# A two-layer graph transformer on one core: lists loaded in two parts, first loads in order of use, the next layer's k and v over four chunks, attention spread at the border

## The chip, the core and the metric

The kernel runs on one core of a Trainium2 chip. The metric is the device time of one launch in microseconds, the median of several runs. The engines are PE (matrix multiplications; PEld is its loading of weights), DVE (elementwise work and reductions), ACT (activations, copies, scaling), POOL (elementwise work, and the issue of gathers and scatters) and SP (issues loads and stores; ACT issues some too).

## What is computed

x has 2708 rows (tokens) of 512 numbers; adj is a 2708 x 2708 matrix of 0 and 1, symmetric, with ones on its diagonal and a few to some twenty ones in a row. Two layers of the same form follow each other, everything in float32:

```python
mask = adj.astype(jnp.float32) + jnp.eye(n, dtype=jnp.float32)
q = (h @ Wq.T + bq).reshape(n, N_HEADS, D_K)      # k and v alike; 8 heads of 64
scores = jnp.einsum('nhd,mhd->hnm', q, k) / jnp.sqrt(jnp.float32(D_K))
scores = jnp.where(mask[None, :, :] == 0, jnp.float32(-1000000000.0), scores)
attn = jax.nn.softmax(scores, axis=-1)
ctx = jnp.einsum('hnm,mhd->nhd', attn, v).reshape(n, D_MODEL)
h1 = _layer_norm(h + ctx @ Wo.T + bo, ln1_g, ln1_b)
ff = jax.nn.relu(h1 @ W1.T + b1) @ W2.T + b2      # 512 -> 2048 -> 512
h2 = _layer_norm(h1 + ff, ln2_g, ln2_b)
```

## The kernel before

The attention goes by edges: for each token only the rows of k and v at the ones of its adjacency row are gathered. Tokens are sorted by the number of ones, most first, into 22 tiles of 128 ranks (the last has 20); `CAPS` gives how many neighbours each tile needs, 22 for tile 0 and 3 for tile 21. `order` is the order of attention: tiles 21 and 20, 19 and 18, 8 and 9, 7 and 10, 6 and 11, 0 and 17, and so on, two tiles a block, 11 blocks.

**First stage** (`first`, L802). For each tile of tokens, in their own order, PE makes k and v (`project`, L564: four products of 128 x 128 by 512 columns) from columns `xg` of x transposed, loaded 256 tokens at a time into three buffers (L811). Beside it `lists` (L649) finds the ones of each adjacency row: SP loads 1354 KB a tile into one of two buffers, POOL adds the diagonal, ACT writes codes, DVE takes the largest codes in segments (L663 to L670). Then `counted` (L678) and `ranked` (L735) make each token's rank; PE adds up over partitions (L742, L749), 22 scatters on POOL's queue (L768) write each token's list to its rank in `rec_d`, and two loads bring the lists back in order of rank: `back` (L779, 21 tiles) and `rest` (L783, 20 rows). A cast on POOL (L794) makes `ident_i` (which token has each rank), and `listed` (L796), on DVE, `idx` and `minus` (the neighbours and their masks).

**First queries** (`first_queries`, L862). PE makes q of the 22 tiles in token order; after the tenth `listed` runs and the pool `pa`, which holds the lists' work, is given back; after the eleventh PE turns the gathered rows `xr` of the first three rank tiles (L1097) and makes their q; attention begins beside the rest of the queries. A gather of q by rank needs all 22 tiles of q stored.

**Main loop** (L1478). For each block `feed_forward` (L1240) runs 16 chunks f: pf, four products of 256 columns (L1265), ACT's relu to ft (L1273), and, `LAG` = 3 chunks later, two products of 512 columns into a (L1253). Beside it run: the attention of later blocks, in steps that `advance(x)` (L1393) lets through: a step has a cost, a credit of at most 1.5 grows by x, and no step is let through while two finished tiles wait in `got`; `through` (L1403) does what is missing of the next block at f = 10, whose context tiles cx are then turned (L1097), projected (o) and normed (`attended`, L1208); and in layer 0 `keys_values` (L1299), the k and v of the layer after for the block just finished, in four pieces: turn the two tiles; k and v of one; k and v of the other; two scatters (L1324). DVE takes k away (L1316), ACT v (L1318).

An attention step: POOL issues gathers of two neighbours of 128 tokens into one of five kv buffers (L951), DVE multiplies by q and adds up (L988, L994), ACT takes the exponent (L1007) and weighs half of the values (L1014), DVE the other half (L1020) and adds (L1027); at a tile's end DVE sums (L1035 to L1050) and ACT divides (L1058).

**The border** (L1450 to L1470). When layer 0 is done, PE makes the first sixteen tiles of layer 1's q (`query`, L1190, evicted by DVE at L1195), the first eight from preloaded zT, the rest from zT that SP loads (L1182), three buffers ahead, behind the stores of the q's (L1205). The first block's attention is let in between by `advance`.

Accumulators in the tag "g" (k, v, q, o, and turned tiles, `ps`) are three. The order on PE, ACT and SP is written out by hand; so is POOL's in the first stage and layer 0, and DVE's in the first queries and at the border. Elsewhere a scheduler orders DVE and POOL.

Of the kernel before, what the change touches and what calls it, by code (L numbers as in the profile page):

```python
# [8 lines left out]
F32 = mybir.dt.float32  # L9
# [37 lines left out]
EARLY = 3  # L47
PACE = (0.62, 0.72)
# [422 lines left out]
def by_edges(ctx: ExitStack, tc: tile.TileContext, x, xT, adj, layers, out, good):  # L471
# [113 lines left out]
    def lists_of(pa):  # L585
# [49 lines left out]
        new = pa.tile([P, NT, 32], F32, tag="new", name="new", bufs=1)  # L635
# [99 lines left out]
        def ranked(hot, before, half):  # L735
# [30 lines left out]
            for t in range(NT):  # L766
# [12 lines left out]
            back = nc.gpsimd.dma_start(  # L779
                out=new[:, : NT - 1, :],  # L780
                in_=rec_d[: (NT - 1) * P, :].rearrange("(g p) c -> p g c", p=P),
            )
            rest = nc.gpsimd.dma_start(out=new[:LW, NT - 1, :], in_=rec_d[(NT - 1) * P :, :])  # L783
            for load in (back, rest):
# [9 lines left out]
            nc.gpsimd.tensor_copy(ident_i, new[:, :, LIST])  # L794

        def listed():  # L796
            nc.vector.tensor_scalar(idx, new[:, :, :LIST], 1.0, 1.0, ALU.max, ALU.subtract)
            nc.vector.tensor_scalar(minus, new[:, :, :LIST], 0.0, NEG, ALU.is_equal, ALU.mult)
# [3 lines left out]
    def first(w, meanwhile):  # L802
# [3 lines left out]
        def load():  # L806
            i = len(xg)
            b = i % XBS * XB
            bw = min(XB, N - b)
            t = wts.tile([P, NC, XB], F32, tag=f"w1_{5 + i % 3}", name="xg")  # L810
            nc.sync.dma_start(out=t[:, :, :bw], in_=chunked(xT)[:, :, b : b + bw])  # L811
            xg.append(t)

        def tokens(t, again):

            i, c0 = t * P // XB, t * P % XB
            if c0 == 0 and len(xg) < 2 * XBS:
                load()
            xs = xg[i + again * XBS]
            return lambda c: xs[:, c, c0 : c0 + size(t)]  # L820

        cols = given_column(w, "bq"), given_column(w, "bk")
        load()
        wk = matrix(w, "Wk", "wk")
        turning = turned_row(cols[1], "bk", 1.0)
# [5 lines left out]
        for t in range(NT):  # L831
# [14 lines left out]
            if t == 0:  # L846
                load()
# [6 lines left out]
            if t == QT:  # L854
                wq = matrix(w, "Wq", "wq")
                turning = turned_row(cols[0], "bq", DK**-0.5)
# [5 lines left out]
    def first_queries(bq, wq, listed, pa, tokens, meanwhile):  # L862
# [15 lines left out]
        for t in range(NT):  # L878
# [10 lines left out]
            if t == OWN - 1:  # L889
                listed()  # L890
# [6 lines left out]
            if t == OWN:  # L897
                zTs = [turned_own(g, xr) for g, xr in zip(order, xrs)]
                for g, zT in zip(blocks[0], zTs):
                    own_query(g, zT, to[g], bq, wq)  # L900
                    advance(0.5)
            if t == OWN + 2:
# [544 lines left out]
    for n in range(NL):  # L1447
        last = n == NL - 1
        nxt = None if last else Layer(n + 1, layers[n + 1])
        if n > 0:  # L1450
# [3 lines left out]
            with tc.manual_schedule(engines={mybir.EngineType.DVE}):  # L1454
# [4 lines left out]
                while pool:  # L1459
                    advance(1.0)  # L1460
                    now.query(*pool.pop(0))
                for i in range(2 * AHEAD - 10):
                    advance(1.0 if i < 3 else 0.4)
# [14 lines left out]
        for k, block in enumerate(blocks):  # L1478
# [4 lines left out]
            for f, zs in enumerate(now.feed_forward(block, hs, hT)):  # L1483
                if f == NFC:
                    break
                if f in (5, 6) and behind:
                    next(behind)
                    if f == 6:
                        for _ in behind:
                            advance(1.0)  # L1490
                        behind = None
# [125 lines left out]
```

## Time and profile before

| | us |
|---|---|
| median of 5 runs | 1974.93 |
| lowest and highest | 1971.67, 1978.03 |
| the profiled execution, whole | 1970.44 |
| its span, first to last instruction | 1968.7 |
| PE busy | 1897.2 |
| DVE, ACT, POOL busy | 1303.2, 933.2, 794.5 |
| kv gathers on POOL's queue (420), busy | 547.5 |
| mean granted clock of PE | 0.986 |

PE's busy time is a union: a matmul counts from its start to a modelled end, and matmuls overlap. A wait line reads "engine line tile <- engine line: us in total, times, longest us". A timeline row is start, length, engine, line, operation, tiles, shapes, how many, and in brackets the idle time before it and what ended it. The granted clock of PE is 1.00 at full speed. In time the stages are: k, v and lists to about 165 us, first queries to 270, layer 0's blocks to 1160, the border to 1235, layer 1 to the end.

### The profile page before, as it was taken

To read this page: it belongs to the slowest core of one execution; us is meant where nothing else is said; L and a number is where in the kernel's file an instruction comes from. 1 tells how busy PE (TensorE), PEld (TensorE's weight loads), DVE (VectorE), ACT (ScalarE), POOL (GpSimd) and SP (SyncE) were. 2 spreads that over 40 slices of the span, in tenths; PEclk is the share of its full clock that TensorE was granted. 3 is DMA by queue.
4 is the path that set the end of the run, shared out by engine and by line. 5 is a ranking of instruction groups with operands and counts; after the bars stand their busy time and mean duration, and the time that the engine had idled before them with its cause. 6 is when DMAs were issued, how large, how long until landed. Compare 5 with 4: busy or idle time off the path is not lost. (4 is left out here: it accounts for less than half of the span.)

```text
span 1968.7 us, 20843 instructions
## 1 busy us (share of the span) xinstructions
PE 1897.2 (96%) x6150; PEld 1099.8 (56%) x6150; DVE 1303.2 (66%) x2139; ACT 933.2 (47%) x3218; POOL 794.5 (40%) x708
## 2 busy tenths in 40 slices
PE   8999989999999999999999997999999999999997
PEld 3443434465565655666556643556666566666664
DVE  6884587585867959659442035887688988877421
ACT  4560344464555655547332112756456765755310
POOL 3114535462555645425310022555346655544210
PEclk9999989999999999999999998999999999999998
DMA  8998767454645656546310755856455766554100
GB/s 328 353 315 283 246 213 257 150 198 157 210 153 194 208 175 222 170 145 210 127 44 22 230 168 203 286 181 214 156 185 190 251 214 211 183 191 150 37 11 13
DMA packets 130942, 366.92 MB, mean 186 GB/s; under 512 B 16636, under 2 KB 36460, under 8 KB 128110
## 3 DMA queue, kind: packets, MB, share of 16 engines
q0 software_dynamic: 69104, 246.35, 37.6%
q1 hardware_dynamic: 52804, 99.66, 14.7%
q10 hardware_dynamic: 8910, 19.48, 2.6%
q8 instruction: 50, 0.82, 0.2%
q14 instruction: 74, 0.61, 0.1%
HBM read 314.62 MB, written 50.83 MB: 186 GB/s over the span
## 5 line engine op out<-in xcount | busy, mean ns | idle before, releaser
L951 POOL DMA_INDIRECT kv<-kv_d,idx x420 | 547.5, 1303 | 488.9 <-DVE acc L1027 332.2
L1253 PE MATMUL a<-w,ft 128*128 128x512 f32 (+1 forms) x1408 | 666.1, 598 | 9.3 <-ACT ft L1273 9.3
L1265 PE MATMUL pf<-hT,w 128*128 128x256 f32 (+1 forms) x2816 | 635.7, 373 | 10.8 <-ACT ft L1273 8.3
L1265 PEld LDWEIGHTS pf<-hT,w 128*128 128x128 f32 x2816 | 520.9, 191 | 188.8 <-issue 107.8
L1253 PEld LDWEIGHTS a<-w,ft 128*128 128x128 f32 (+1 forms) x1408 | 256.0, 186 | 233.9 <-issue 198.1
L1273 ACT ACTIVATE ft<-pf,b 128x256 f32<-128x256 f32 (+1 forms) x352 | 157.6, 458 | 426.3 <-PE pf L1265 425.8
L988 DVE TENSOR_TENSOR kv<-kv,q 128x1024 f32<-128x1024 f32 (+3 forms) x222 | 256.3, 1157 | 139.3 <-DMA kv<-kv_d,idx 130.5
L1014 ACT ACTIVATE kv<-kv,p 128x64 f32<-128x64 f32 x1232 | 311.0, 335 | 5.0
L994 DVE TENSOR_REDUCE sc<-kv 128x16 f32<-128x1024 f32 (+3 forms) x222 | 254.6, 1152 | 1.1
L1027 DVE TENSOR_TENSOR acc<-acc,kv 128x1024 f32<-128x1024 f32 (+2 forms) x178 | 203.7, 1144 | 35.7 <-ACT kv L1014 35.2
L1087 POOL TENSOR_TENSOR rd<-va,mhalf 128x1 f32<-128x1 f32 (+1 forms) x88 | 85.6, 973 | 278.6 <-DVE va L1085 277.2
L1007 ACT ACTIVATE p<-sc,minus 128x8 f32<-128x8 f32 (+1 forms) x420 | 103.4, 295 | 167.8 <-DVE sc L994 159.9
L1020 DVE TENSOR_TENSOR kv<-kv,p 128x512 f32<-128x512 f32 (+1 forms) x178 | 121.3, 682 | 72.2 <-ACT p L1007 72.2
L568 PE MATMUL o<-wo,cT 128*128 128x512 f32 (+1 forms) x352 | 155.1, 593 | 0.5 <-ACT cT L1102 0.5
L568 PEld LDWEIGHTS o<-wo,cT 128*128 128x128 f32 (+1 forms) x352 | 65.1, 186 | 86.5 <-issue 74.7
L1058 ACT ACTIVATE cx<-acc,su 128x64 f32<-128x64 f32 (+1 forms) x352 | 88.5, 334 | 42.7 <-DVE su L1050 34.7
L1285 DVE TENSOR_TENSOR h<-a,h 128x512 f32<-128x512 f32 (+1 forms) x44 | 29.7, 677 | 106.3 <-PE a L1253 106.1
L1091 DVE SCALAR_TENSOR_TENSOR h<-h,rd,ln_b 128x512 f32<-128x512 f32 (+1 forms) x88 | 65.8, 747 | 49.2 <-POOL rd L1087 49.2
L660 ACT ACTIVATE code<-aj 128x2708 bf16<-128x2708 int32 (+1 forms) x22 | 73.2, 3330 | 47.7 <-POOL aj L656 44.1
L663 DVE MAX8 tops<-code 128x8 f32<-128x247 f32 (+2 forms) x242 | 82.9, 401 | 17.6 <-ACT code L660 17.6
L1014 ACT ACTIVATE acc<-kv,p 128x64 f32<-128x64 f32 (+1 forms) x352 | 88.8, 334 | 1.4
L1324 POOL DMA_INDIRECT kv_d<-kvs,ident_i x22 | 23.1, 1051 | 162.5 <-ACT kvs L1318 95.4
(132 smaller groups left out, 1512.9 us busy)
## 6 DMA issues: line engine op xcount, KB each, us to landing
aj<-in_adj SPq DMA_DIRECT2D x21, 1354.0 KB, 7.3
kv_d<-kvs ACTq DMA_DIRECT2D x21, 512.0 KB, 6.9
xg<-in_xT SPq DMA_DIRECT2D x20, 512.0 KB, 5.8
w<-in_W SPq DMA_DIRECT2D x20, 512.0 KB, 4.8
kv<-kv_d,idx POOLq DMA_INDIRECT x420, 5.6
w<-in_W ACTq DMA_DIRECT2D x12, 512.0 KB, 6.1
q_d<-qs SPq DMA_DIRECT2D x22, 256.0 KB, 3.1
zT_d<-zT SPq DMA_DIRECT2D x22, 256.0 KB, 3.4
```

Source lines behind the costliest of these rows:

```text
L568: nc.tensor.matmul(o[:r], xs(c), wm[:, c, :], start=(c == 0), stop=(c == NC - 1))
L951: nc.gpsimd.indirect_dma_start(out=to, out_offset=None, in_=table[:, :], in_offset=bass.IndirectOffsetOnAxis(ap=s, axis=0), bounds_check=N ...
L988: nc.vector.tensor_tensor(kv[:r, :c, :DM], kv[:r, :c, :DM], self.q[:r].unsqueeze(1).to_broadcast([r, c, DM]), ALU.mult,)
L994: nc.vector.tensor_reduce(self.sc[:r, s0 : s0 + c, :], kv[:r, :c, :DM].rearrange("p s (h d) -> p s h d", d=DK), AX.X, ALU.add,)
L1007: nc.scalar.activation(p[:r, s, :], self.sc[:r, s, :], AF.Exp, bias=minus[:r, g, s : s + 1])
L1014: nc.scalar.activation(to[:, i, hd], kv[:r, i, DM + h * DK : DM + (h + 1) * DK], AF.Copy, scale=p[:r, s0 + i, h : h + 1],)
L1020: nc.vector.tensor_tensor(to[:, 0, :].rearrange("p (h d) -> p h d", d=DK), kv[:r, 0, DM:].rearrange("p (h d) -> p h d", d=DK), p[:r, s0, : ...
L1027: nc.vector.tensor_tensor(self.acc[:r, :c, :], self.acc[:r, :c, :], kv[:r, :c, DM:], ALU.add)
L1058: nc.scalar.activation(cx[:r, hd], self.acc[:r, 0, hd], AF.Copy, scale=self.su[:r, h : h + 1])
L1253: nc.tensor.matmul(a[:r], fts[f][:, c0 : c0 + r], self.w2[f // 2][:, f % 2, :], start=(f == 0), stop=(f == NFC - 1),)
L1265: nc.tensor.matmul(pf[:, :w], self.w1[f // 2][:, c, f % 2 * P : f % 2 * P + P], hT[:, c, :w], start=(c == 0), stop=(c == NC - 1),)
L1273: nc.scalar.activation(ft[:, :w], pf[:, :w], AF.Relu, bias=self.b1[:, f : f + 1])
```

## The change

Five edits. (1) `back` becomes a function and the lists come in three loads: first `rest`, then the three tiles before it, then the other 18; a cast for the last four tiles follows, and `listed` is called twice, for four tiles after the tenth query and for 18 after the twelfth, with a second cast on POOL. (2) Because the lists now outlive the pool `pa`, `new` lies in the buffer of `hT`. (3) The first loads: half of xg (128 tokens), the first quarter of Wk, the column bk, the rest of Wk, the column bq, the other half of xg; before, both columns, all of xg, all of Wk. (4) `keys_values` is stepped once at each of f = 5, 6, 7 and 8; before, once at 5 and all the rest at 6, with three `advance(1.0)` that go. (5) At the border each query or streamed step lets `advance(0.65)` through; before 1.0, and 0.4 from the fourth streamed step on.

```diff
--- before.py
+++ after.py
@@ -45,6 +45,7 @@
 QT = 6
 OWN = 10
 EARLY = 3
+FIRST = 4
 PACE = (0.62, 0.72)
 
 
@@ -632,7 +633,9 @@
             base=0,
             channel_multiplier=-1,
         )
-        new = pa.tile([P, NT, 32], F32, tag="new", name="new", bufs=1)
+        new = dn.tile([P, NC, 2 * P], F32, tag="hT", name="new", bufs=1)
+        new = new.rearrange("p c t -> p (c t)")[:, : NT * 32]
+        new = new.rearrange("p (g c) -> p g c", c=32)
         nc.gpsimd.memset(new, 0.0)
         nc.gpsimd.dma_start(
             out=rec_d[: (NT - 1) * P, :].rearrange("(g p) c -> p g c", p=P),
@@ -776,12 +779,16 @@
                 tc.declare_no_dep(move.ins, group="moved", reason="no two tokens have one rank")
                 tc.add_to_no_dep_group("moved", move.ins)
                 moved.append(move)
-            back = nc.gpsimd.dma_start(
-                out=new[:, : NT - 1, :],
-                in_=rec_d[: (NT - 1) * P, :].rearrange("(g p) c -> p g c", p=P),
-            )
-            rest = nc.gpsimd.dma_start(out=new[:LW, NT - 1, :], in_=rec_d[(NT - 1) * P :, :])
-            for load in (back, rest):
+            def back(a, b):
+                load = nc.gpsimd.dma_start(
+                    out=new[:, a:b, :],
+                    in_=rec_d[a * P : b * P, :].rearrange("(g p) c -> p g c", p=P),
+                )
+                return load
+
+            first, last = NT - FIRST, NT - 1
+            rest = nc.gpsimd.dma_start(out=new[:LW, last, :], in_=rec_d[last * P :, :])
+            for load in (rest, back(first, last), back(0, first)):
                 for move in moved:
                     tc.add_manual_dep(
                         load.ins,
@@ -791,11 +798,16 @@
                         ),
                         reason="every list is in its place",
                     )
-            nc.gpsimd.tensor_copy(ident_i, new[:, :, LIST])
-
-        def listed():
-            nc.vector.tensor_scalar(idx, new[:, :, :LIST], 1.0, 1.0, ALU.max, ALU.subtract)
-            nc.vector.tensor_scalar(minus, new[:, :, :LIST], 0.0, NEG, ALU.is_equal, ALU.mult)
+            nc.gpsimd.tensor_copy(ident_i[:, first:], new[:, first:, LIST])
+
+        def listed(start):
+
+            ts = slice(NT - FIRST, NT) if start else slice(0, NT - FIRST)
+            if not start:
+                nc.gpsimd.tensor_copy(ident_i[:, ts], new[:, ts, LIST])
+            some = new[:, ts, :LIST]
+            nc.vector.tensor_scalar(idx[:, ts, :], some, 1.0, 1.0, ALU.max, ALU.subtract)
+            nc.vector.tensor_scalar(minus[:, ts, :], some, 0.0, NEG, ALU.is_equal, ALU.mult)
 
         return lists, counted, ranked, listed
 
@@ -808,21 +820,32 @@
             b = i % XBS * XB
             bw = min(XB, N - b)
             t = wts.tile([P, NC, XB], F32, tag=f"w1_{5 + i % 3}", name="xg")
-            nc.sync.dma_start(out=t[:, :, :bw], in_=chunked(xT)[:, :, b : b + bw])
             xg.append(t)
+            step = bw if i else P
+            for a in range(0, bw, step):
+                nc.sync.dma_start(
+                    out=t[:, :, a : a + step], in_=chunked(xT)[:, :, b + a : b + a + step]
+                )
+                yield
 
         def tokens(t, again):
 
             i, c0 = t * P // XB, t * P % XB
             if c0 == 0 and len(xg) < 2 * XBS:
-                load()
+                finish(load())
             xs = xg[i + again * XBS]
             return lambda c: xs[:, c, c0 : c0 + size(t)]
 
-        cols = given_column(w, "bq"), given_column(w, "bk")
-        load()
-        wk = matrix(w, "Wk", "wk")
-        turning = turned_row(cols[1], "bk", 1.0)
+        wk = wts.tile([P, NC, DM], F32, tag="wk", name="wk")
+        halves = load()
+        next(halves)
+        for c in range(NC):
+            nc.sync.dma_start(out=wk[:, c, :], in_=chunked(w["Wk"])[:, c, :])
+            if c == 0:
+                cols = [given_column(w, "bk")]
+        cols.append(given_column(w, "bq"))
+        finish(halves)
+        turning = turned_row(cols[0], "bk", 1.0)
         bk = next(turning)
         wv = matrix(w, "Wv", "wv")
         pa = tc.tile_pool(name="pa", bufs=2)
@@ -844,7 +867,7 @@
                 nc.scalar.dma_start(**before)
             before = dict(out=kv_d[0][t * P : t * P + r, :], in_=kv[:r])
             if t == 0:
-                load()
+                finish(load())
             while done < min(NT, 1 + LEAD * t):
                 lists(done)
                 done += 1
@@ -853,7 +876,7 @@
             meanwhile(t)
             if t == QT:
                 wq = matrix(w, "Wq", "wq")
-                turning = turned_row(cols[0], "bq", DK**-0.5)
+                turning = turned_row(cols[1], "bq", DK**-0.5)
                 bq = next(turning)
                 finish(turning)
         nc.scalar.dma_start(**before)
@@ -887,7 +910,7 @@
                 qs[:r, t % 2], q[:r], DK**-0.5, bq[:r], ALU.mult, ALU.add
             )
             if t == OWN - 1:
-                listed()
+                listed(True)
                 pa.__exit__(None, None, None)
                 at = ctx.enter_context(tc.tile_pool(name="at", bufs=2))
                 for g in order[:3]:
@@ -899,6 +922,8 @@
                 for g, zT in zip(blocks[0], zTs):
                     own_query(g, zT, to[g], bq, wq)
                     advance(0.5)
+            if t == OWN + 1:
+                listed(False)
             if t == OWN + 2:
                 own_query(order[2], zTs[2], to[order[2]], bq, wq)
             meanwhile(t)
@@ -1457,10 +1482,10 @@
                 next(ahead)
                 next(streamed)
                 while pool:
-                    advance(1.0)
+                    advance(0.65)
                     now.query(*pool.pop(0))
                 for i in range(2 * AHEAD - 10):
-                    advance(1.0 if i < 3 else 0.4)
+                    advance(0.65)
                     next(streamed)
                 through(0)
                 early[n] = now.attended(blocks[0], got)
@@ -1483,12 +1508,8 @@
             for f, zs in enumerate(now.feed_forward(block, hs, hT)):
                 if f == NFC:
                     break
-                if f in (5, 6) and behind:
+                if f in (5, 6, 7, 8) and behind:
                     next(behind)
-                    if f == 6:
-                        for _ in behind:
-                            advance(1.0)
-                        behind = None
                 if more and f == 10 + (k + n == 0):
                     through(k + 1)
                     projecting = now.attended(blocks[k + 1], got)
```

## The prediction

> **What bounds the kernel now.** I read the busy row of the page first, then the list of who waited for whom on the matmul engine, then the table by stretches of time, and last the timelines around the longest waits. The busy row:
>
> ```profile
> PE 1897.2 (96%) x6150; PEld 1099.8 (56%) x6150; DVE 1303.2 (66%) x2139; ACT 933.2 (47%) x3218; POOL 794.5 (40%) x708
> ```
>
> PE does something 96% of the span, so 1968.7 − 1897.2 = 71.5 us are idle, 13 of them the store at the end. No other engine is near full over the span. The time can only go where PE stands still, or where it runs at a lower clock. The waits of PE, longest in total first:
>
> ```profile
> PE a L1253 <- ACT ft L1273: 9.3, 9, 2.8
> PE q L568 <- DVE qs L1195: 8.7, 2, 5.9
> PE pf L1265 <- ACT ft L1273: 8.3, 3, 5.9
> PE v L568 <- DVE kvs L1316: 6.4, 2, 4.6
> PE k L568 <- DMA wk<-in_Wk: 6.3, 1, 6.3
> ...
> PE tp L1097 <- DMA xr<-in_x,ident_i: 3.5, 3, 2.7
> PE pr L742 <- DVE kvs L838: 3.4, 1, 3.4
> ```
>
> Four of these are touched: the start (6.3), the first lists (3.5), the next layer's k and v (6.4), the queries at the border (8.7). The table by stretches shows what stands beside them; columns: stretch, length, then busy time of PE, PEld, DVE, ACT, POOL, the granted clock of PE, DMA share and rate.
>
> ```profile
> 155.00:170.00 15.00, 11.61 (x31) 4.19 (x30) 8.91 (x33) 0.91 (x2) 3.98 (x4) 1.00 0.77 263
> 204.00:220.00 16.00, 12.45 (x32) 4.69 (x31) 3.79 (x4) 1.56 (x4) 10.95 (x11) 0.79 0.72 218
> 371.00:383.00 12.00, 7.40 (x13) 3.04 (x12) 5.73 (x8) 0.75 (x2) 0.94 (x1) 0.72 0.12 41
> 1186.00:1207.00 21.00, 11.36 (x18) 4.18 (x16) 14.66 (x23) 5.13 (x21) 7.91 (x6) 0.76 0.67 235
> ```
>
> After three of the four waits the clock falls (0.79, 0.72, 0.76) and the matmuls that follow take longer, so a wait costs more than its own length. After the wait of 3.39 us at 158 it stayed at 1.00. Rows of the timelines:
>
> ```profile
> 195.10 1.50 POOL L779 DMA_DIRECT2D new<-rec_d  x1 [1.65 <-DMA rec_d<-rec,ranks]
> 203.19 0.48 POOL L794 CAST ident_i<-new 128x22 int32<-128x22 f32 x1 [6.02 <-DMA new<-rec_d]
> 207.86 0.58 PE L1097 MATMUL tp<-ident,xr 20*128 20x20 f32 x4 [2.70 <-DMA xr<-in_x,ident_i]
> 376.58 6.21 PE L568 MATMUL v<-wv,zT 128*128 128x512 f32 x8 [4.60 <-DVE kvs L1316]
> 375.85 1.26 DVE L1316 TENSOR_TENSOR kvs<-k,bk 20x512 f32<-20x512 f32 x2
> 1200.57 5.53 PE L568 MATMUL q<-wq,zT 128*128 128x512 f32 x8 [5.88 <-DVE qs L1195]
> 1199.88 1.82 DVE L1195 SCALAR_TENSOR_TENSOR qs<-q,bq 128x512 f32<-128x512 f32 x3
> ```
>
> A projection is 3.44 us from start to start at the full clock (k at 149.83 to v, and on); the 6.21 and 5.53 above are the same work at the lower clock. In the built order of both programs PE has the same instructions; only the k and v of the second tile of each layer-0 block move behind one feed-forward chunk.
>
> **First loads.** Before, two columns (0.79 and 1.24) stand ahead of the 512 KB of xg (1.71) and of Wk (2.18); PE starts at 6.34. Now half of xg is first at 0.79: 0.92 us sooner, and 256 KB less ahead of the first matmul, 0.8 us at the 328 GB/s of slice 1 of the page: PE starts near 4.6, some 1.7 us sooner. SP issues one DMA more (0.4 us) ahead of the adjacency loads; the bytes ahead of them are the same. That does not reach the end: at 158.25 PE waits for the list chain on DVE (L838 and what stands ahead of it), whose adjacency loads keep DMA at 0.90 to 0.93. An earlier PE only waits longer, 3.39 + 1.7 − 0.5 = 4.6 us. I give the chain 0.5 us from DMA having started sooner (bounds −0.4, the extra issue, and 0.9). The longer wait may now bring the clock down: nothing by the 3.39 row, 6.21 − 3.60 = 2.6 us by the 4.60 row; I take 1.2, about midway, as 4.6 equals the one length but the other is the same place. Together 0.5 − 1.2: 0.7 us lost.
>
> **Lists.** The cast waits for one load of 336 KB and one of 2.5 KB behind it, until 203.19. Now 2.5 KB (issue 0.58) and 48 KB (at most 0.7) go first, then 288 KB (at most 1.5); the cast wants the first two but stands behind the third's issue, so not before 195.10 + 2.8 = 197.9. Landing of the short ones: between the 3.5 us of a gather of xr and the 6.5 us that the 2.5 KB load took, so 195.10 + 1.3 + 3.5 to 6.5 = 199.9 to 202.9, since the queue's neighbours (q_d, xg) load DMA just then. I take 200.2, nearest to xr, which goes through the same queue beside the same loads: 3 us sooner. The three xr land 3 us sooner, the last near 207.2; PE arrives at 205.16 and waits about 1 us instead of 3.55, and the loss by clock goes mostly: from 205.16 to 219.96 are 14.8 us for 0.3 + 2 × 0.43 + 2 × 3.44 = 8.0 us of work, 6.8 lost. I take 5.0 won, less 0.6 because the second part of the lists puts 0.8 us of DVE (432 of the 528 columns of 0.44 + 0.45) in the stretch 224 to 242 that ends at PE's `tp<-cx` at 244.09 without slack. 4.4 us; bounds 0 (the load lands no sooner) and 6.8. POOL's second cast (0.4) stands behind four gathers; its load has long landed.
>
> The Trainium skill, DMA: Bandwidth & Descriptors, section "Anatomy of one DMA — SWDGE (gpsimd) path", speaks against this part: it puts a load at about 2.0 us fixed plus bytes over 436 GB/s, so 336 KB would take 2.8 us and 48 KB 2.1, an estimate of 0.7 us saved, and the whole sum would be some 4 us smaller. The rows here (7.8 us for the 336 KB, 6.5 for 2.5 KB behind it) do not follow it, so I keep to them.
>
> **k and v of layer 1.** There are three accumulators under the tag of k and v, so the second v waits until the first k is taken away by DVE L1316 at 375.85 to 376.5. DVE is held there by gathers (waits of 6.32, 0.92 and 0.36 us for kv before it), not by PE. With a chunk (pf and a, 3.44 us) between, PE reaches that v at 375.4 and waits 1.1 us. Before, from the end of the second k at 371.98 to 382.63 are 10.65 us for 3.44 of work; after, 1.1 + 3.44 when the clock holds: 6.1 us won. DVE's chain behind it moves by only about 3 us (it waits for ACT's p, which waits for the copy of v and for the scatter that POOL issues at 383.69), and it must reach `h` for `tp<-h` at 421.36; its last L1091 is at 415.92 to 416.7, so 4.7 us of slack take the 3 us difference. I take 5.5; bounds 2 and 7.2. At 703.10 the wait of 1.79 is shorter than the new chunk and goes: 1.8 (bounds 0 and 1.8). The scatter comes two chunks later; POOL's gathers stand behind it.
>
> **Attention in layer 0.** Three `advance(1.0)` go in each block. The built order of ACT moves attention in blocks 1 and 4 only. In block 4 the last two steps of the long tile (22 lists) now stand behind the third ft: ft at 633.5, then p and eight Copies twice (2.5 each) and cx (2.0) end near 640.5; before, cx ended at 640.61. Nothing, bounds −3.4 and +3.4 (a chunk).
>
> **Border.** Three accumulators again. DVE did the sixth q at 1199.88 and held PE 5.88 us; in the built order it comes right behind the fifth, at 1189.2, and the seventh after nine instructions, near 1197.9. The first wait (2.85) stays. From 1194.7 PE then runs on to 1201.3, and waits for the zT of the ninth streamed load: SP issues it behind the store of the seventh q, near 1198.7, and it lands 4.9 us later, 1203.6. Before, the same projection began at 1207.26 + 3.44 = 1210.7: 7.1 us; I take 7.0. Bounds 4 (another store's wait) and 9 (no wait).
>
> **Sum**: −0.7 + 4.4 + 5.5 + 1.8 + 0 + 7.0 = 18.0 us. From the profiled execution's 1970.44 us that gives 1952.4; the median of the runs, 1974.93, lies 4.5 above it, and gives **1957**. The rest behaves as before: the wait of 5.93 at 277 hangs on the last first-layer query, its store and its gather, in the same order.
>
> The Trainium skill, TensorE: Matmul & The Clock Gate, section "HAM oscillation — how this bites in real kernels", warns of gaps above about 3.4 us only. The wait of 2.70 us that is followed by 0.79 differs from it; by the rule the lists and the first wait at the border would cost nothing but their length, and only the wait at 158, now above 3.4, would be charged: a sum smaller by about 4 us.
>
> **Rivals.**
> *The short load lands no sooner* (the 6.5 row): the change doesn't do there what it says. 18.0 − 4.4 = 13.6: 1961.
> *Given back*: DVE is busy 46.07 of 50 us from 400 to 450, so PE, earlier, meets the attention chain and waits for ft or h there; the lists and k, v give nothing, the border stays (DVE is idle from 1218 on but for PE's own). 7.0 − 0.7: 1969.
> *Slower*: attention falls behind for want of the three advances and is done in one burst at chunk 10 of each layer-0 block, PE waiting at `tp<-cx`. The row is 635.49: 3.73 of wait, then 1.91 and 3.62 for 0.5 and 1.89: 6.8 a block. It decides from three blocks (18.0 / 6.8 = 2.6); with four 1957 + 27 = 1984. Against it: the order of ACT is changed in two blocks.
>
> **Numbers.** Forecast 0.50 (1949 to 1960 by its own bounds); short load 0.17; given back 0.18; slower 0.07; more than forecast (all bounds high, about 1946) 0.08. The range 1946 to 1970 leaves out the slower case and a tail of the others. A measurement tells 0.2%, 4 us, from no change: faster 0.87 (all of the first, second and last, and two thirds of the third), same 0.06, slower 0.07.
>
> **What would show it.** PE's first matmul near 4.6 us; a longer wait at `pr` L742, and the clock behind it; the first cast near 200; no `tp<-xr` wait above 1.5; at the first L1316 a wait of about 1 us, no wait near 703; at the border one wait of 2.9 and one near 2 for zT. I am wrong if PE's waits at `tp<-cx` or ft in blocks 1 to 9 grow by more than those shrink.

## The result, and the profile after

The changed kernel takes 1971.09 us, the median of 23 runs (1966.42 to 1978.34), beside 1975.18 of 43 runs of the kernel before: a ratio of 0.9978, interval 0.9971 to 0.9986, 4.1 us less. Run twice more, on two chips, it lay 8.8 us (0.9946, 0.9932 to 0.9959) and 4.9 us (0.9975, 0.9960 to 0.9990) below before. Faster, then, but by a quarter to a half of the 18 us forecast. The profiled execution took 1964.43 us with a span of 1962.6, 6.0 less than before's. In the changed kernel the lines have moved on by 1 to 25: L568 is L569, L742 L745, L838 L861, L1195 L1220, L1316 L1341, L1265 L1290, L1273 L1298.

The busy row, and the list of who waited for whom on PE (us in total, times, longest):

```profile
PE 1898.0 (97%) x6150; PEld 1100.3 (56%) x6150; DVE 1301.3 (66%) x2141; ACT 933.6 (48%) x3218; POOL 790.9 (40%) x710
```

```profile
PE a L1278 <- ACT ft L1298: 9.5, 9, 2.8
PE pf L1290 <- ACT ft L1298: 9.0, 3, 5.9
PE tp L1122 <- ACT cx L1083: 5.2, 2, 3.8
PE k L569 <- DMA wk<-in_Wk: 4.6, 1, 4.6
PE pf L1290 <- ACT hT L1127: 4.6, 5, 2.3
PE tp L1122 <- DMA xr<-in_x,ident_i: 3.6, 2, 2.5
PE q L569 <- DMA zT<-zT_d: 3.3, 2, 2.7
PE q L569 <- DVE qs L1220: 3.1, 1, 3.1
PE pr L745 <- DVE kvs L861: 3.0, 1, 3.0
PE v L569 <- DVE kvs L1341: 2.8, 2, 2.0
PE a L1278 <- DVE va L1110: 1.6, 1, 1.6
...
```

PE's idle time fell from 71.5 to 1962.6 − 1898.0 = 64.6 us. The first loads came as forecast (6.3 to 4.6). The wait for xr did not go (3.5 to 3.6). At the border 8.7 became 3.1, with 3.3 for zT behind it (1.2 before). At v 6.4 became 2.8, but two lines are new or longer: `a` waits 1.6 for DVE, and pf waits 4.6 for hT (2.6 before). The same four stretches in the table by stretches of time (length, PE, PEld, DVE, ACT, POOL, clock, DMA share and rate):

```profile
155.00:170.00 15.00, 12.03 (x29) 4.59 (x28) 7.62 (x28) 0.57 (x1) 3.92 (x4) 0.89 0.78 240
204.00:220.00 16.00, 12.37 (x32) 4.76 (x31) 3.79 (x4) 1.40 (x3) 9.86 (x11) 0.79 0.81 255
371.00:383.00 12.00, 11.20 (x31) 5.60 (x30) 5.33 (x6) 3.56 (x14) 2.57 (x3) 1.00 0.11 38
1186.00:1207.00 21.00, 16.58 (x33) 6.72 (x34) 15.65 (x25) 4.33 (x17) 4.61 (x4) 0.92 0.81 282
```

At the first k and v the clock now holds (0.72 before) and PE is nearly full (11.20 of 12 us); at the border it is 0.92 (0.76). At the lists nothing changed (0.79 twice). Since PE has the same matmuls in both kernels, its progress can be laid side by side. This is when PE starts the same matmul, worked out from the two traces (for the own queries it is the sixth of their matmuls):

```
                                      before    after    sooner by
first k                                 6.34     4.59       1.75
ranks (pr)                            161.64   160.18       1.46
own queries of the rank tiles         215.04   215.30      -0.26
h of block 1 turned                   334.47   334.10       0.37
behind the first k and v              387.58   380.89       6.69
one block later                       464.85   462.08       2.77
ahead of the k and v at 703           672.81   671.27       1.54
behind them                           713.38   709.89       3.49
one block later                       795.15   792.68       2.47
border                               1184.98  1182.57       2.41
behind the border                    1214.20  1206.51       7.69
layer 1, block 3                     1558.42  1552.54       5.88
```

So the k and v were won (6.3 us) and mostly lost again within one block, the lists brought nothing in this pair, and the border 5.3 us.

### The profile page after: what moved, and what is told of

Same layout as the page of the kernel before. It is cut to its first block, busy times and chain, and to the rows that moved or that the text cites. A ratio compares the mean times of both kernels' runs of the same rounds, so it can differ in the third digit from the quotient of the medians.

```text
span 1962.6 us, 20851 instructions
## 1 busy us (share of the span) xinstructions
PE 1898.0 (97%) x6150; PEld 1100.3 (56%) x6150; DVE 1301.3 (66%) x2141; ACT 933.6 (48%) x3218; POOL 790.9 (40%) x710
## 5 line engine op out<-in xcount | busy, mean ns | idle before, releaser
L976 POOL DMA_INDIRECT kv<-kv_d,idx x420 | 541.5, 1289 | 476.7 <-DVE acc L1052 316.4
L1290 PE MATMUL pf<-hT,w 128*128 128x256 f32 (+1 forms) x2816 | 637.6, 373 | 13.6 <-ACT ft L1298 9.0
L1290 PEld LDWEIGHTS pf<-hT,w 128*128 128x128 f32 x2816 | 521.5, 191 | 192.4 <-issue 106.9
L1298 ACT ACTIVATE ft<-pf,b 128x256 f32<-128x256 f32 (+1 forms) x352 | 158.5, 459 | 432.4 <-PE pf L1290 432.0
L569 PE MATMUL o<-wo,cT 128*128 128x512 f32 (+1 forms) x352 | 155.1, 593 | 0.5 <-ACT cT L1127 0.5
L569 PEld LDWEIGHTS o<-wo,cT 128*128 128x128 f32 (+1 forms) x352 | 65.1, 186 | 86.5 <-issue 74.5
```

Source lines behind the costliest of these rows:

```text
L569: nc.tensor.matmul(o[:r], xs(c), wm[:, c, :], start=(c == 0), stop=(c == NC - 1))
L976: nc.gpsimd.indirect_dma_start(out=to, out_offset=None, in_=table[:, :], in_offset=bass.IndirectOffsetOnAxis(ap=s, axis=0), bounds_check=N ...
L1290: nc.tensor.matmul(pf[:, :w], self.w1[f // 2][:, c, f % 2 * P : f % 2 * P + P], hT[:, c, :w], start=(c == 0), stop=(c == NC - 1),)
L1298: nc.scalar.activation(ft[:, :w], pf[:, :w], AF.Relu, bias=self.b1[:, f : f + 1])
```

## The experiments

One trace is one execution, and stretches differ from one to the next by chance. So I set the same marks in the traces of all runs below and give means over the kernels with and without an edit (range in brackets):

```
stretch                            without the edit     with it              change
start to the own queries (1-3)     216.7 (214.5-220.1)  214.5 (212.1-217.4)  -2.2
h of block 1 to behind k, v (4)     53.0 (51.8-54.2)     47.6 (46.6-49.6)    -5.4
the block after (4)                 77.3 (76.8-77.7)     82.6 (81.1-85.6)    +5.2
on to 672 (4)                      208.5 (208.0-209.5)  209.7 (209.2-210.6)  +1.2
around the k and v at 703 (4)       41.1 (40.3-42.6)     38.8 (38.6-39.0)    -2.3
the block after (4)                 81.8 (81.8-81.8)     84.1 (82.7-84.7)    +2.3
border (5)                          30.2 (29.2-30.9)     24.2 (22.6-26.4)    -6.0
```

Row 1 has 4 traces without and 12 with the edits (a standard error of 1.4 us on the difference), the rows of edit 4 six and nine, the border four and nine. `kv_adv` and the lighter kernels stay out of the rows of edit 4, the quiet ones out of row 1, and the lighter kernels and those with other zT loads out of the border. Edit 4 sums to +1.0 with a standard error of 0.9: nothing is won. The table comes to −2.2 + 1.0 − 6.0 = −7.2 us. What lies between its rows differs by +0.3 (own queries to block 1) and +0.2 (795 to the border), and layer 1 behind the border takes 1.0 us longer in the kernels with edit 5 (standard error 0.6; the last section says where). That leaves about 5.7, within the measured 4.1 to 8.8.

**The parts alone.** `loads_lists` is the changed kernel with edits 4 and 5 undone; `kv_only` and `border_only` are the kernel before with one edit; `no_kv` is the changed kernel with edit 4 undone.

```diff
--- kv_only against before (no_kv: the same, backwards)
-                if f in (5, 6) and behind:
+                if f in (5, 6, 7, 8) and behind:
                     next(behind)
-                    if f == 6:
-                        for _ in behind:
-                            advance(1.0)
-                        behind = None
--- border_only against before (loads_lists: this and the first, backwards)
-                    advance(1.0)
+                    advance(0.65)
...
-                    advance(1.0 if i < 3 else 0.4)
+                    advance(0.65)
```

> Only the first loads and the lists of the change (edits 1 to 3); k, v and the border as before. Theory one (these edits bring nothing to PE, as its lead at 210 us shows): 1975, within 1.5 us of before. Rival (they bring the 3.7 us of the forecast, and the changed kernel loses that in layer 0 by the other edits): 1971.

Measured: 1974.05 us, ratio 0.9986 (0.9971 to 1.0001), 2.3 below before. Between the theories; not told from no change.

> The kernel before with edit 4 alone (k and v over four chunks, no advance between). Theory one (6.3 us are won at the first k and v, and DVE, which runs attention at its own pace, takes back near 4 in the next block): lead of PE 6 to 7 us at 390, 2 to 3 at 470, median 1972 to 1973. Rival (the loss in the next block comes from the other edits' moves, not from this one): lead still above 5 at 470, median 1968 to 1970. Second rival (the three advances are missed: waits at tp<-cx in later blocks): a lead that falls block by block, median 1975 or more.

Measured: 1973.28 us, 0.9986 (0.9972 to 1.0000). Its trace ran 5 us behind before's from the first stage on, so the leads must be read as differences: 5.2 behind at 340, 0.6 ahead behind the first k and v, 5.4 behind one block later. What is won there is lost in the next block by edit 4 alone: the first theory, not the rival. The median lies 3.1 below before, at the edge of its interval, while the stretches of edit 4 sum to nothing won; the two are not reconciled.

> The kernel before with edit 5 alone (0.65 of attention per query at the border). Theory one (the border's gain stands by itself): PE 5 to 6 us ahead at 1215, median 1969 to 1971, waits there of about 3.0 for the eviction of q and 2.7 and 0.6 for zT. Rival (layer 1's own attention takes part of it back by its clock or its waits): lead 5 to 6 at 1215 but under 4 at the end, median 1972.

Measured: 1970.29 us, 0.9971 (0.9959 to 0.9982), 6.0 below before, border 24.7 us. Of the 4.5 us that its trace wins at the border 4.3 are there at the last matmul, so the rival fell. One edit alone does what the whole change does.

> The changed kernel without edit 4 (k and v in two pieces and three advances, as before). Theory one (edit 4 wins 5.3 us at the first k and v and 3.1 at 703, and loses as much in the blocks behind them): within 2 us of the changed kernel, 1968 to 1972, 4 to 9 below before. Rival (edit 4 is worth the 2.8 us that it showed alone): 1972 to 1974, 2 to 5 below before.

Measured: 1965.96 us, 0.9953 (0.9937 to 0.9970), 8.9 below before, as the changed kernel itself on that chip (8.8). The change is no worse without edit 4.

**Lists.** In the first trace of the changed kernel the short loads are early and the cast comes at 201.45 (203.19 before), but the rows xr do not. Loads in the window 194 to 212, with the median time to landing:

```profile
new<-rec_d POOLq DMA_DIRECT2D x1, 288.0 KB, 5.6
...
new<-rec_d POOLq DMA_DIRECT2D x1, 48.0 KB, 5.4
xr<-in_x,ident_i POOLq DMA_INDIRECT x3, 4.8
new<-rec_d POOLq DMA_DIRECT2D x1, 2.5 KB, 1.8
```

Before, xr took 3.5 us; now, issued 1.7 us sooner, they take 4.8. Timeline rows of that trace:

```profile
195.37 0.59 POOL L790 DMA_DIRECT2D new<-rec_d  x1 [2.28 <-DMA rec_d<-rec,ranks]
195.95 2.10 POOL L783 DMA_DIRECT2D new<-rec_d  x2
201.45 0.19 POOL L801 CAST ident_i<-new 128x4 int32<-128x4 f32 x1 [3.40 <-DMA new<-rec_d]
206.42 0.39 PE L1122 MATMUL tp<-ident,xr 20*128 20x20 f32 x4 [1.08 <-DMA xr<-in_x,ident_i]
209.36 1.94 PE L1122 MATMUL tp<-ident,xr 128*128 128x128 f32 x8 [2.55 <-DMA xr<-in_x,ident_i]
```

The full rank tiles are turned at 209.36, before at 209.01. By the packets of the trace, SP's store of q and its load of xg, 1 MB together, move at 203 to 207 in the changed kernel, and nearly all packets of xr behind them, at 207 to 209; the 48 KB load, issued at about 196, moves at 200, behind the pair before it (196 to 200).

This pair of traces is not like the others. The second trace of the same kernel, `after_again`:

```profile
197.04 0.59 POOL L790 DMA_DIRECT2D new<-rec_d  x1 [1.62 <-DMA rec_d<-rec,ranks]
200.12 0.19 POOL L801 CAST ident_i<-new 128x4 int32<-128x4 f32 x1 [0.41 <-DMA new<-rec_d]
197.09 0.69 DVE L909 SCALAR_TENSOR_TENSOR qs<-q,bq 128x512 f32<-128x512 f32 x1 [10.79 <-remote]
199.29 0.37 SPq L895 DMA_DIRECT2D q_d<-qs  x1
207.25 5.37 PE L569 MATMUL q<-wq,xg 128*128 128x512 f32 x8 [2.47 <-DMA xg<-in_xT]
212.54 1.44 PE L1122 MATMUL tp<-ident,xr 20*128 20x20 f32 x12
```

From the first load's issue to the cast it takes 3.1 us (6.1 in the first trace), and PE turns xr without a wait. But DVE stood idle for 10.8 us ahead of a q, SP's store of that q came late, the load of xg behind the store with it, and PE waits 2.5 us for xg. The others go the same way: issue to cast takes 2.9 to 3.1 us in all twelve other traces with the lists in parts and 5.4 to 5.8 in the four others without (8.1 in the first), and PE waits for xr in none of the twelve. Where all of xg is loaded, it waits for xg instead, 1.6 to 3.5 us. Without the edit the waits for xr and xg together are 2.9 to 5.6.

`burst_late` puts SP's store and load at 203 behind the own queries (`held[0]` is `load`, which is not called at t == OWN then).

```diff
-            if t % 2 == 0 and made:
+            if t % 2 == 0 and made and t != OWN:
                 written()
...
                     advance(0.5)
+                written()
+                finish(held[0]())
```

> The changed kernel, but SP's store of q 8 and 9 and its load of the next xg (1 MB together, moving from 203.5 to 208 us in the changed kernel) are issued behind the first two rank tiles' q instead of ahead of the eleventh token tile's. Theory one (the rows xr, whose gathers the earlier lists do issue 1.7 us sooner, wait for SP's burst): the second and third xr land near 207 to 208 instead of 209.3, PE is about 2 us ahead of the changed kernel by 215, and the median is 0 to 3 us below 1971, according to what layer 0 takes back. Theory two (the gathers wait in their own queue behind the 288 KB of the third list load, or are that slow by themselves): second xr at 209.3 as before, nothing gained by 215, median 1971.

Measured: 1969.46 us, 0.9960 (0.9943 to 0.9976). PE did not wait for xr, as in the other traces; it stood earlier, for xg:

```profile
PE q L569 <- DMA xg<-in_xT: 3.4, 1, 3.4
```

At the mark in the own queries PE was 1.2 us ahead of the changed kernel's first trace. The next pair leaves three loads of xg out, and with them both their traffic and PE's wait for them:

```diff
         def load():
             i = len(xg)
+            if i in (16, 17, 18):
+                xg.append(xg[i - 3])
+                return
```

> The kernel before without three of the second loads of xg (1.5 MB between 189 and 208 us); the queries of token tiles 10 to 15 are made from the columns of tiles 4 to 9 instead. Theory one (the list loads, xr and xg wait for each other on the DMA engines): the list load lands by 200 instead of 203.2, xr by 205, PE waits there 1 us or less instead of 2.3 to 3.6, and the stretch from the first ranks to the own queries takes 43 to 46 us instead of 48 to 51; of that, 2 to 5 us may be lost again at 277 and 333. Rival (the lists are slow by themselves, by the chain of scatters, load, cast and gathers): cast at 202 or later, the wait for xr above 2, the stretch 48 us or more.

> The changed kernel without the same three loads. Theory one: no wait for xr or xg there above 0.5, stretch 43 to 45 us, and no more than 2 us sooner than the pair's other kernel, since without the traffic the whole list is early enough. Rival: the lists in two parts now show the 3 to 4 us of the forecast against the pair's other kernel.

Measured: 1973.37 and 1964.24 us (0.9995, 0.9983 to 1.0008; 0.9947, 0.9931 to 0.9962): 9.1 us apart, where the full kernels on that chip are 4.9 apart. From the ranks to the first own query PE took 48.6 us in the one, with 1.8 us of wait for xr, and 45.3 in the other, with none (49.8 and 51.1 in the first traces of the full kernels). Neither theory has it whole. The changed kernel came near the 43 to 45 of the first, and its waits for xr and xg, 1.6 to 3.6 us in the traces with all loads, are gone. But the kernel before missed its 43 to 46, cast only at 203.7, and the two parts show 3.3 us, as the rival said. From issue to cast the lists take 5.6 and 3.0 us here, as in the other traces with all loads, so there the traffic of xg did not hold them. By these two traces the lists bring their gain where PE has no xg to wait for; with it the table has 2.2, standard error 1.4, edit 3 included. Whether xg is late by SP's place in the order or by the DMA engines, the pair does not tell.

**k and v.** The rows of DVE that hold PE one block after the first k and v in the changed kernel, and the two waits of PE:

```profile
428.50 1.23 DVE L1013 TENSOR_TENSOR kv<-kv,q 128x1024 f32<-128x1024 f32 x1 [1.73 <-DMA kv<-kv_d,idx]
429.64 0.18 DVE L1108 BATCH_NORM_AGGREGATE mv<-st 128x2 f32<-128x6 f32 x1
429.73 0.66 DVE L1310 TENSOR_TENSOR h<-a,h 128x512 f32<-128x512 f32 x1
...
430.44 1.13 PE L1278 MATMUL a<-w,ft 128*128 128x512 f32 x2 [1.56 <-DVE va L1110]
458.54 3.70 PE L569 MATMUL v<-wv,zT 128*128 128x512 f32 x8 [2.02 <-DVE kvs L1341]
```

The same read in the kernel before:

```profile
429.86 0.67 DVE L1285 TENSOR_TENSOR h<-a,h 128x512 f32<-128x512 f32 x1
```

DVE stands at a multiplication whose gather has not landed, and the read of the second accumulator comes behind it, at 429.73; before, it came at 429.86, the same time, while PE is 4.9 us ahead. `kv_adv` puts the three advances back, which gives DVE's order of before from 401 us on in this block; `adds_first` reads both accumulators ahead of both norms.

```diff
--- kv_adv against after
                 if f in (5, 6, 7, 8) and behind:
                     next(behind)
+                    if f > 5:
+                        advance(1.0)
--- adds_first against after
+            for g, a, h in zip(block, accs, hs):
+                r = size(g)
+                nc.vector.tensor_tensor(h[:r], a[:r], h[:r], ALU.add)
             for g, a, h in zip(block, accs, hs):
                 r = size(g)
                 z = h
-                nc.vector.tensor_tensor(z[:r], a[:r], h[:r], ALU.add)
                 norm(z, r, self.g2, self.e2)
```

> The changed kernel with the three advance(1.0) of each layer-0 block put back, one behind each of the pieces at f = 6, 7 and 8. In the built order DVE then has the order of the kernel before in the block after. Theory one (the loss of 4 to 6 us in the block after the first k and v comes from the removed advances: a step of attention moves, and DVE's order there changes): no wait of PE for the norm near 429, none above 1 us for k at 456, 77 to 78 us for that block instead of 81, PE 6 us ahead of before at 465, and the median 4 us less than the changed kernel's, 1967. Theory two (attention runs at its own pace, and a PE that is earlier meets it in any order): 81 us or more for that block, PE 2 to 3 us ahead at 465, median 1971.

Measured: 1976.53 us, 1.0005 (0.9992 to 1.0018): all of the gain gone. The block after took 86.9 us. My first theory, the order, fell. The waits near 429 and 456 did go; in their place PE waits for the norm of the next block's h at 412 and 414, and again near 660 and 666 (the stretches 400 to 425 and 655 to 690):

```profile
PE tp L1122 <- DVE h L1116: 4.2, 2, 2.9
...
PE tp L1122 <- DVE h L1116: 10.1, 2, 5.7
```

The second theory has the block right (81 or more) but not the rest: PE is level with before at 465, not 2 to 3 us ahead, and the median lies 5 above its 1971.

> The changed kernel, with the second residual's adds of both tiles ahead of both norms (the accumulators are read first, the rest as it was). Theory one (DVE's order holds PE twice: 1.56 at the second accumulator, near 429, then 2.0 and a clock at k, near 456, by the kv buffers that come free late): the wait near 429 falls to 0.5 or less, the one near 456 stays 2 to 3.6, the block's 81 us by at most 1.5 shorter, median 1970 to 1971. Rival (both waits follow from the late accumulator): both go, block 78 us, median 1967.

Measured: 1966.12 us, 0.9939 (0.9926 to 0.9953), on the chip where the changed kernel itself gave 0.9946. The wait at the accumulator stayed 1.56 and the one at v 2.73; the block took 83.3. The scheduler put the second read behind the same multiplication, so the edit did not do what it says and tells nothing apart.

The two lighter kernels take attention work off DVE, ACT and the gathers there:

```diff
+LESS = {9: 4, 7: 4, 10: 4, 6: 4}
...
     def chunks_of(g):
-        S = CAPS[g]
+        S = CAPS[g] - LESS.get(g, 0)
...
```

> The kernel before, with four neighbours left out in the attention of each of the rank tiles 6, 7, 9 and 10 in both layers (their scores, weights and sums take the first lists only), so that DVE, ACT and the gathers have less to do beside blocks 1 and 2. It is the base for the next one: all theories expect the waits at v (4.6 near 372) and at the border as before, and 77 to 78 us or less for the stretch behind the first k and v.

> The changed kernel with the same neighbours left out. Theory one (attention on DVE, at its own pace, takes the first k and v's gain back in the next block): with the lighter attention the stretch behind the first k and v takes no more than 1 us longer than in the kernel before with the same left out (81 to 86 against 77 to 78 without), the gain of 5 us there stays, and the two lie 9 to 12 us apart. Rival (the split itself costs it: the kv buffer that holds k and v is held for two chunks more, the scatter comes two chunks later and the gathers stand behind it): the stretch is again 4 us or more longer, and the two lie 4 to 8 us apart as the full kernels do.

Measured: 1983.28 us (1.0044, 1.0027 to 1.0061) and 1974.51 (0.9998, 0.9988 to 1.0008), 8.8 apart. Both end some 7 us later behind the last matmul; why is open. The block after the first k and v took 76.81 us in both, where the full kernels differ by 5.2: with less attention the gain at the first k and v (3.0 us here) stays, and in `after_lite` PE waits for nothing between 340 and 500. That is the first theory. But at 746 to 757 `after_lite` waits 2.05 for h and 3.67 for hT, and that block takes 88.1 us against 81.8: PE meets attention later, not never. The rival, that the split itself holds a kv buffer longer, does not show in the first block; but with fewer neighbours fewer buffers are wanted too, so it is not ruled out.

**Border.**

```diff
--- zT_act against after
...
-                    nc.sync.dma_start(out=zT, in_=zT_d[self.n][tiles[len(zTs)]])
+                    by.dma_start(out=zT, in_=zT_d[self.n][tiles[len(zTs)]])
...
-            streamed = now.queries(order[8 : 2 * AHEAD])
+            streamed = now.queries(order[8 : 2 * AHEAD], nc.scalar)
--- zT_five against after
...
-                while len(zTs) < min(i + 3, len(tiles)):
+                while len(zTs) < min(i + 3 + more, len(tiles)):
+                    if more and len(zTs) in (3, 4):
+                        if len(zTs) == 3:
+                            two = dn.tile([P, NC, 2 * P], F32, tag="hT", name="zT2", bufs=1)
...
-            streamed = now.queries(order[8 : 2 * AHEAD])
+            streamed = now.queries(order[8 : 2 * AHEAD], 2)
```

> The changed kernel with the streamed zT loads of the border issued by ACT instead of SP. Theory one (they stand behind the stores of q on SP): the waits of 2.7 and 0.6 us for zT go, the border takes 20.5 to 22 us instead of 24, median 1968. Rival (a zT load waits for its buffer, which PE frees, and then takes its 2 us; or it waits on ACT behind attention): border 24 us or more, median 1971 to 1973.

Measured: 1974.12 us, 0.9986 (0.9976 to 0.9995), border 28.1 us, the wait for zT 5.86: the rival. Behind attention on ACT the load is later still.

> The changed kernel with five zT loads ahead of the border's streamed queries instead of three: two more lie in the two halves of the buffer of hT, which is idle there, so no zT load stands behind the stores that hold PE at 1199 to 1206. Theory one (the load behind the store is what PE waits for): both zT waits go, the border takes 20.5 to 22 us instead of 24, median 1965 to 1968 (before as 1975 to 1977). Rival (DVE is next: an attention step between two evictions holds the accumulator): a wait for the eviction of q of 2 to 3 us takes its place, 23 to 25 us, median as the changed kernel's.

Measured: 1961.87 us, 0.9938 (0.9921 to 0.9955), the lowest median of all, 13 below before; border 19.4 us. PE's waits in the window 1180 to 1216, where the changed kernel had 3.3 for zT and 3.1 for the eviction:

```profile
PE q L569 <- DVE qs L1227: 4.5, 3, 2.3
PE o L569 <- ACT cT L1127: 0.7, 2, 0.5
```

No zT wait is left, and no half clock follows. What remains is DVE's evictions, 4.5 us, as the rival said, but not in place of the gain.

> The changed kernel without edit 4 and with five zT loads ahead at the border. Theory one (edit 4 is worth nothing, the zT waits cost 4.5 us of the border): border 19 to 20 us instead of 24, median 3 to 6 us below the changed kernel on this chip, 10 to 14 below before. Rival (edit 4 is worth something beside the others): no better than the 13 us below before of the kernel with edit 4 and five loads.

Measured: 1964.75 us, 0.9955 (0.9938 to 0.9972), border 19.3 us, 10.4 below before and 5.5 below the changed kernel on that chip. With edit 4 or without it, the version with five loads beats the kernel before and takes 4 to 5 us less at the border than the changed one. `zT_five` against the changed kernel on its chip is not told apart by the ratios (0.9938 and 0.9946).

**The change itself again**, for the spread (no edit):

> The changed kernel itself once more, for a second trace of it and a time on the same chip as the next three. All theories: 1971, within 1.5 us against before as first measured (4.1 less). In the trace, what belongs to the program comes again: 46 to 48 us from the first turned h of block 1 to the chunk behind k and v, 81 us or more for the block after, 24 us for the border. What hangs on chance differs: which of xg and xr PE waits for at 200 to 210 us, and the half-clock stretch at 1536.

> The changed kernel for the third time. If its gain is what the stages of the traces show (border 5 to 6, lists and first loads 0 to 2, k and v about 0), 5 to 8 us below before; below 4.5 or above 8.5 would leave the two first sets apart by the chip.

Measured: 1967.86 and 1970.26 us, the ratios above. The stretches came again (k and v 49.6 and 47.9, the block after 84.1 and 81.4, border 23.9 and 23.7). The sum of the stretches, about 5.7, lies between the sets; why these differ by 4.7 us stays open.

## Why the prediction was right and wrong

By the means of the traces, some 6 us were won instead of 18.0. Of the 12 missing, 8.3 are k and v (7.3 forecast, 1.0 lost), 1.5 the first loads and lists (3.7 and 2.2), 1.0 the border (7.0 and 6.0), and 1.0 lies in layer 1, of which "the rest behaves as before" was said.

*Direction and border: right.* The border was to give 7.0 and gives 6.0 (5.3 in the profiled pair). The mechanism was the forecast one: the 5.88 goes. The term was mis-sized at "waits for the zT ... near 1198.7, ... 1203.6": the waits for zT are 2.71 and 0.57, not one of 2.3, and the first wait for the eviction 3.11 instead of 2.85; `zT_five`, with its loads ahead, has no zT wait.

*k and v: the two gains right, the sum wrong.* 5.5 was taken for the first and 5.4 measured; 1.8 for the one at 703 and 2.3 measured. The failed step is "4.7 us of slack take the 3 us difference", with "the rest behaves as before". I followed DVE to one deadline, `tp<-h` at 421, and found slack there. Attention goes on at its own pace, so a PE that stays 6 us ahead meets the next deadline, the second accumulator at 429 (1.56 us), and the next, k at 456 (2.02). It gives back 5.2 + 1.2 + 2.3 = 8.7 us. That edit 4 alone does this is shown by `kv_only`; that attention's pace is the reason rests on one lighter pair and these rows. The rival *given back* named it and its row, DVE's 46.07 of 50 us, though it looked for the waits at ft or h; its 1969 is nearest to the median. I gave it 0.18.

*Attention in layer 0: nothing, as forecast*, in the sense that the advances are not missed: put back, they cost more. The waits at cx did not grow (5.4 to 5.2 in all).

*Lists: the early load right, its worth wrong.* The short load was to land 3 us sooner. From issue to cast it is 2.0 us less in the profiled pair and some 2.6 in the others, contrary to that rival. The step that failed is "PE arrives at 205.16 and waits about 1 us instead of 3.55". It prices the wait for xr alone, and PE has a second one at that place, for xg. In the first trace of the changed kernel xr moved behind SP's store and load and came no sooner; in the others xr was there in time and PE waited for xg, 1.6 to 3.5 us. I had named these neighbours and priced them for the list load only. Of 4.4 − 0.7 = 3.7 for edits 1 to 3, 2.2 are measured (standard error 1.4, so 3.7 is not excluded); in the profiled pair, nothing.

*First loads: PE at 4.59, as forecast, and worth little.* The full clock comes at 10.3 us instead of 9.6, so of the 1.75 us 0.54 are left when k is done. That time is chance too: 8.5 to 11.6 in the traces with the edit, 9.6 to 11.2 without. The wait at `pr` was forecast to grow to 4.6; it was 2.97 there, and 2.97 to 4.46 in the other traces with the edit, 2.50 to 4.46 without. So it did not grow. The clock fell behind it, as forecast, but by luck: it falls in 8 of 13 traces with the edit and in 4 of 5 without; the kernel before's first trace is the exception. The last section says why.

The Trainium skill, DMA: Bandwidth & Descriptors, section "Anatomy of one DMA — SWDGE (gpsimd) path", had spoken against the lists, and they did give less, but not for its reason: its estimate of 0.7 us saved stands against 2.0 to 2.6 us from issue to cast. Its rule agrees with the 2.5 KB load (an estimate of 2.0 us, 1.8 measured) but not with the 48 and 288 KB behind it (2.1 and 2.7 estimated, 5.4 and 5.6 measured), which stood beside SP's bursts; in `after_again` the cast came 2.5 us behind the issue of the 48 KB.

## What to carry to other kernels

Before a stall is priced as a gain, ask what else runs at its own pace beside it: the engine that comes earlier meets every later deadline of the slower chain, not only the first, so follow it for a whole block. A load that is made early helps only as far as nothing else that the engine needs at that place comes late: here, with the rows in time, it stood for its own columns. And make one trace per edit: the largest edit alone (the border) gave as much as the five together, and one of them could be left out.

## What the runs showed of the hardware

In these runs the clock of PE is set on a fixed grid. In all 18 traces the half-clock stretches last 3.41 us or a multiple of it (3.41, 6.83, 10.24), but for the last, behind the final matmuls, and in each trace their edges lie on one grid of 3.413 us, to within 0.004. I counted PE's idle time in each cell at full clock: with 2.1 us idle or more, the next cell was at half clock in 121 of 121 cases; with 1.8 to 2.1 in 19 of 46; with 1.4 to 1.8 in 5 of 85; with 0.7 to 1.4 in none of 146. So not the length of a wait decides but how much of it falls into one cell. The 3.39 us at 158 in the kernel before were cut by an edge into 1.6 and 1.8 and cost nothing more; the 2.97 in the changed kernel lay in one cell and brought the clock down. The Trainium skill, TensorE: Matmul & The Clock Gate, section "HAM oscillation — how this bites in real kernels", speaks of gaps above about 3.4 us; here 2.1 within one cell were enough.

Where the grid lies against the program differs from trace to trace, so this is also chance. One wait of about 1.5 us near 1540, the same in both kernels, was followed by a half-clock cell in 10 of the 18 traces: the stretch of layer 1 around it takes 314.0 to 314.1 us or 315.7 to 315.9 in 13 of them, half a cell apart. Such a cell comes in nine of thirteen traces with the border's edit and in one of five without, too few to say that the edit has no part. In the profiled pair 1.7 us of it went against the change (5.9 us sooner behind it, 7.7 ahead).

In all traces but the first pair, DVE also stands idle for 6 to 11 us between 181 and 200, while POOL issues its scatters; what holds it there is open.
